# Cross-attention block on one Trainium2 core: low score products in one run, context in bank 3, low masks first, empty PE instructions shared between W2 and W1

## The chip, the cores and the metric

The kernel runs on one NeuronCore of a Trainium2 chip. The metric is the device time of one execution in microseconds. Before the change the median of 3 runs is 1749.11 us (1749.05 to 1751.23). TensorE is called PE here, VectorE DVE, ScalarE ACT, GpSimd POOL; SP issues most DMAs.

## What is computed

A cross-attention block with its feed-forward part, in fp32, for 128 sequences of 128 tokens, 256 features, 16 heads of 16, and 1024 hidden units. The reference, cut to what matters:

```python
q, k, v = query @ Wq + bq, key @ Wk + bk, values @ Wv + bv   # split into 16 heads
scores = einsum('bhqd,bhkd->bhqk', q, k) / sqrt(16)
scores = where(j < i, scores, -1e30)          # a query sees earlier keys only
attn = softmax(scores); attn[:, :, 0, :] = 0  # the first query sees none
x = layer_norm(query + ctx @ Wo + bo, ln1_g, ln1_b)
ffn = relu(x @ W1 + b1) @ W2 + b2
out = layer_norm(x + ffn, ln2_g, ln2_b)
```

## The kernel before

The work goes in 64 pairs of sequences, p = 0 to 63. All five engines follow an order written out by hand: a function call in the kernel adds its instructions to each engine's queue at that place, and a tile framework adds only the semaphore waits. Pairs 0 to 4 have orders of their own (the start, `third`, `fourth`, `fifth`); from p = 5 on `step(p)` is called for each pair, and at the end `behind` twice and a few calls more. The pipeline is deep: `step(p)` computes the context of pair p-2, scores and softmax of pair p, the queries and keys of p+1, the hidden layer of p-3 and the second feed-forward product of p-4.

On PE a step runs in this order: the context products (`weigh`, L583 and L594), the scores (`scores_both`), queries (L271, `xT,wq`), output projection (L614), keys (L271, `cT,wk`), values (L303), the second feed-forward product W2 (`second_by_seven`, L891), and the hidden layer W1 (`hidden`, L801). An fp32 matmul is carried out as two matmul instructions with a weight load each, so counts in the profile are twice those in the order.

The scores use the mask. Query rows 64 to 127 are two groups of 32 (g = 2 with 96 keys, g = 3 with 128 keys), called high (HI); rows 0 to 63 are one group with 64 keys, called low (LO, g = 0). Low products are 16 matmuls of 64 rows (`low_products`, L423), high ones 16 for each g of 32 rows (`group_scores`, L406). Each uses a strip of 32 of PE's rows (`strips`, r = 0 to 3). Four of the eight PSUM banks hold the high scores (bank r for strip r), the other four the low ones (bank 4 + (r + 2) % 4). `scores_both` mixes them: low products of strips 2 and 3 for half of the heads, high ones of g = 3 in strips 0 and 1, low ones again, and so on.

DVE then adds the masks. For low scores `masked(p, 0, FORE)` reads banks 4 and 5 and `masked(p, 0, REAR)` banks 6 and 7 into SBUF (L455). For high ones `mask_high` adds the mask in place (L843) and takes each head's maximum from PSUM (L459), for strips 0 and 1 (FORE) or 2 and 3 (REAR). ACT takes the exponentials: 16 of the high heads straight from the banks, 16 of the low ones from SBUF (`exponential_by_head`, L857).

The banks are used again within a step: queries in bank 4, output projection in 5, keys in 0, values in 1, W1 in banks 2, 3, 4 and 0 in turn, W2 in 6 and 7, and `weigh` puts the context into bank 7, from where ACT copies it to `cxT` (`context`, L607). A matmul that writes a bank waits until the engine that read it last is done.

W2 multiplies by the 2 x 2 blocks of W2 in seven products of 4 matmuls (`product`), the four sums that it needs (`hS`) come from POOL (`combine_hidden`, L877 to L880), and DVE adds the products up (`sum_of_seven`, L920 and L928). After its matmuls stand empty instructions (`empty`, L225): 20 in each of five products and 19 in two, 138 in all, 5 after a matmul nearly everywhere. They compute nothing:

```python
    def empty(n):
        for _ in range(n):
            nc.tensor.nop(hint="pad", nofuse=True)
```

W2 is called this way 60 times, for pairs 3 to 62.

Of the kernel before, what the change touches and what calls it, by code (L numbers as in the profile page):

```python
# [13 lines left out]
P = 128  # L14
# [5 lines left out]
def tile_cross_attention_block(  # L20
# [162 lines left out]
    one = const.tile([1, P], F32, tag="one", name="one")  # L183
# [36 lines left out]
    def at_bank(i, name):  # L220
        return banks[:, i, :]
# [5 lines that stand above are left out]
    def bank(name):  # L227
        turns[0] += 1
        return at_bank(4 + turns[0] % 4, name)
# [185 lines left out]
    def low_products(p, strips=range(NS), ms=range(KC)):  # L415

        st = states[p]
        bank0 = 4 if p > 3 else 0
        for m in ms:
            for s in range(2):  # L420
                for r in strips:
                    strip, first = slice(32 * r, 32 * r + 32), s * P
                    nc.tensor.matmul(  # L423
                        banks[s * HP : (s + 1) * HP, bank0 + (r + 2) % 4, m * P : (m + 1) * P].rearrange(
                            "p (e j) -> p e j", e=2
                        ),
                        st["qT"][strip, m, first : first + HP],
                        st["kT"][strip, m, :, first : first + HP],
                        start=True, stop=True,
                    )  # L430

    def scores_both(p):

        one, two = (0, 1), (2, 3)
        low_products(p, two, (0,))
        group_scores(p, 3, one)
        low_products(p, two, (1,))
        group_scores(p, 3, two)
        group_scores(p, 2, one)
        low_products(p, one, (0,))  # L440
        group_scores(p, 2, two)
        low_products(p, one, (1,))

    def masked(p, g, at=slice(0, 4)):

# [11 lines left out]
    def largest(p, g, src=None, heads=slice(None)):  # L457
        src = weights(p, g) if src is None else src
        nc.vector.tensor_reduce(  # L459
            states[p]["nmx"][g][:, heads], src, AX.X, ALU.max, negate=True  # L460
        )
# [110 lines left out]
    def weigh(p):  # L572

        st = states[p]
        pT = st.pop("pT")
        pc = at_bank(7, f"pc_{p}") if p > 1 else bank(f"pc_{p}")
        new = p > 1

        for m in range(KC):
            for s in range(2):  # L580
                at = (m * 2 + s) * P
                for j in range(NS):
                    nc.tensor.matmul(  # L583
                        pc[32 * j : 32 * j + 32, at : at + HP],
                        st["vd"][:, s, 4 * m + j].rearrange("p e d -> p (e d)"),
                        pT[:, 2 * s : 2 * s + 2, 1, 2 * ((j + 2) % 4) + m, :] if new
                        else pT[:, 2 * s : 2 * s + 2, H + 2 * j + m, :],
                        start=True, stop=True,
                    )
            for s in range(2):  # L590
                at = (m * 2 + s) * P
                for e in range(2):
                    for j in range(NS):
                        nc.tensor.matmul(  # L594
                            pc[32 * j : 32 * j + 32, at + HP : at + P],
                            st["vz"][:, s, 4 * m + j, 2 * e : 2 * e + 2, :].rearrange(
                                "p e d -> p (e d)"
                            ),
                            pT[:, 2 * s + m, 0::2, 2 * j + e, :] if new
                            else pT[:, 2 * s : 2 * s + 2, 4 * j + 2 * m + e, :],  # L600
                            start=(e == 0), stop=(e == 1),
                        )
        st["pc"] = pc
# [186 lines left out]
    def hidden(p, fs, between=None):  # L790
        st = states[p]
        if fs[0] == 0:
            st["hT"] = ffn.tile([P, FC, TP], F32, tag="hT", name=f"hT_{p}", bufs=1)
        for f in fs[::2]:
            if p == 0:
                ph = bank(f"ph_{p}_{f}")
            else:
                ph = at_bank((2, 3, 4, 0)[f // 2], f"ph_{p}_{f}")
            for i in range(2):
                for k in range(KC):  # L800
                    nc.tensor.matmul(  # L801
                        ph[:, i * TP : (i + 1) * TP].rearrange("p (s i a) -> p s i a", s=2, a=32),
                        w1[:, k, (f + i) * P : (f + i + 1) * P], st["x1T"][:, :, :, k, :],
                        start=(k == 0), stop=(k == KC - 1),
                    )
            for i in range(2):
                nc.scalar.activation(  # L807
                    st["hT"][:, f + i, :], ph[:, i * TP : (i + 1) * TP], AF.Relu,
                    bias=(b1e_c if p else b1_c)[:, f + i : f + i + 1], scale=1.0,
                )  # L810
            if between:
                between(f)
# [36 lines left out]
    HI, LO = (3, 2), (0,)  # L849
# [11 lines left out]
    wt = const.tile([P, 4, FC // 2, P], F32, tag="wt", name="wt")  # L861
# [20 lines left out]
    def second_by_seven(p):  # L882

        st = states[p]
        hT, hs = st["hT"], st["hS"]
        py = st["py"] = at_bank(6, f"py_{p}")
        pz = st["pz"] = at_bank(7, f"pz_{p}")

        def product(out, left, right, after):
            for k in range(FC // 2):  # L890
                nc.tensor.matmul(  # L891
                    out, left(k), right(k), start=(k == 0), stop=(k == FC // 2 - 1)
                )
                empty(after // (FC // 2) + (after % (FC // 2) > k))

        def raw(e, s):
            return lambda k: hT[:, 2 * k + e, s * P : (s + 1) * P]

        def weights(e, h):
            return lambda k: w2[:, 2 * k + e, h * P : (h + 1) * P]  # L900

        product(py[:, :P], raw(0, 0), weights(0, 0), 20)
        product(pz[:, :P], raw(1, 0), weights(1, 0), 20)
        product(pz[:, 2 * P : 3 * P], raw(1, 1), lambda k: wt[:, 3, k], 20)
        product(py[:, 3 * P :], lambda k: hs[:, 0, k], lambda k: wt[:, 0, k], 20)
        product(py[:, 2 * P : 3 * P], lambda k: hs[:, 2, k], lambda k: wt[:, 2, k], 20)
        product(py[:, P : 2 * P], lambda k: hs[:, 1, k], lambda k: wt[:, 1, k], 19)
        product(pz[:, P : 2 * P], lambda k: hs[:, 3, k], weights(1, 1), 19)

    def sum_of_seven(p):  # L910

# [324 lines left out]
    def step(p):  # L1236
        last = p == NP - 1
        weigh(p - 2)
        context(p - 2)
        if p == 5:  # L1240
            second_sum(1)
        scores_both(p)
        if p > 6:
            combine_hidden(p - 4, POOL_ALONE)
        if p == 5:
            finish(0)
            store(0)
        add_bo(p - 1)
        load_ahead(p)
        for g in LO:  # L1250
            masked(p, g, FORE)
        mask_high(p, FORE)
        exponential_by_head(p, HI, ONES)
        mask_high(p, REAR)
        exponential_by_head(p, HI, TWOS)
        for g in LO:
            masked(p, g, REAR)
        for g in LO:
            largest(p, g)
        if p > 5:  # L1260
            exponential_by_head(p, LO, range(H))
        if not last:
            queries(p + 1)
        attention_out(p - 2)
        attention_sum(p - 2)
        attention_stats(p - 2)
        shift(p - 2, 1)
        norm1(p - 2)
        if not last:
            keys(p + 1)  # L1270
        if p == 5:
            exponential_by_head(p, LO, range(H))
        values(p)
        values_out(p)
        if p > 5:
            norm2(p - 5)
        divided(p, 3)
        divided(p, 2)
        divided(p, 0)
        turn_x1(p - 2)  # L1280
        residual1(p - 3)
        if p > 6:
            second_by_seven(p - 4)
        elif p == 6:
            second_half(2, 1)
        hidden(p - 3, range(FC // 2 if p == 5 else 0, FC))
        if p == 5:
            second_half(2, 0)
        if p + 2 < NP:
            tokens(p + 2, "x")  # L1290
            tokens(p + 2, "c")
        turned(p, 3)
        if p > 6:
            sum_of_seven(p - 4)
        for g in (2, 0):
            turned(p, g)
        brought(p, nc.sync, LATE_FIRST)
        if p > 5:
            finish(p - 5)
            store(p - 5)  # L1300
        stats(p - 4, states[p - 4]["t2"], 2)
        scale_and_shift(p - 4)
# [101 lines left out]
```

## Time and profile before

| what | value |
|---|---|
| median of 3 runs | 1749.11 us (1749.05 to 1751.23) |
| the profiled execution | 1748.55 us |
| its span, first to last instruction | 1746.8 us |
| granted PE clock | 0.997 of full speed |
| PE busy | 1722.8 us |
| DVE, ACT, POOL busy | 1271.8, 1103.6, 1246.9 us |
| DMA, mean | 110 GB/s |

A row of a timeline names the start and the length in us, the engine, the line, the operation, the tiles it writes and reads, their shape and the number of instructions merged in it; in brackets stands the engine's idle time before it and what ended that. Matmuls are pipelined and their ends are modelled, so a row's length reaches into the next row, and the difference of two starts is the better measure. `PEld` is PE's weight load; a `q` behind an engine's name is its sequencer.

### The profile page before, as it was taken

Reading aid. Unit: us, or ns where it says so; the run is one execution under the profiler, and the core shown is the slowest. Engines: PE = TensorE matmul, PEld = TensorE weight load, DVE = VectorE, ACT = ScalarE, POOL = GpSimd, SP = SyncE. Lnnn points to the kernel's source line nnn. Section 1 sums busy time; section 2 is a strip of 40 time slices with the busy share of each in tenths; the row PEclk is TensorE's granted clock in tenths of the full one; section 3 lists DMA queues with packets and bytes.
Section 4 is the critical chain, followed back from the end, with each engine's and each line's share of the span. In section 5 each row is a group of like instructions: output and inputs, shape, how many; then the busy total and the mean of one; then the engine's idle time right before and its main releaser. Section 6 shows DMA issues by size and latency. Waiting matters only on the chain.

```text
span 1746.8 us, 58786 instructions
## 1 busy us (share of the span) xinstructions
PE 1722.8 (99%) x19910; PEld 1419.0 (81%) x19910; DVE 1271.8 (73%) x2240; ACT 1103.6 (63%) x3391; POOL 1246.9 (71%) x1297
## 2 busy tenths in 40 slices
PE   8989999999999999999999999999999999999998
PEld 6767888888888888888888888888888888888787
DVE  7767787687777777866876877777778678778654
ACT  6556576676675665765766766656657667667542
POOL 7856776776777777767767767777777677677664
PEclk9999999999999999999999999999999999999999
DMA  8354455454454454454554554544545545543321
GB/s 176 81 119 114 115 116 122 109 114 113 106 119 116 110 119 104 110 124 109 117 113 104 115 122 108 119 106 108 121 113 113 114 105 119 123 105 92 95 64 43
DMA packets 415325, 192.75 MB, mean 110 GB/s; under 512 B 282448, under 2 KB 387024, under 8 KB 415056
## 3 DMA queue, kind: packets, MB, share of 16 engines
q1 hardware_dynamic: 413152, 188.03, 46.6%
q8 instruction: 189, 3.10, 0.8%
q10 hardware_dynamic: 1904, 0.96, 0.2%
q14 instruction: 80, 0.66, 0.1%
HBM read 70.26 MB, written 33.29 MB: 59 GB/s over the span
## 4 chain that ended last, share of the span: by engine, by line
PE 95%; DVE 1%; POOL 1%; ACT 1%; DMA 1%; issue 0%; SPq 0%; POOLq 0%; ACTq 0%; DVEq 0%
PE banks L891 27%; PE banks L801 26%; PE banks L271 13%; PE banks L614 6%; PE banks L303 6%; PE banks L406 5%; PE banks L423 5%; PE banks L594 3%; PE banks L583 2%; PE banks L819 0%; ACT sm L857 0%; DMA pT<-tb 0%; POOL sm L548 0%; DVE nmx L459 0%; SPq L506 0%
## 5 line engine op out<-in xcount | busy, mean ns | idle before, releaser
L801 PE MATMUL banks<-x1T,w 128*128 128x256 f32 x2048 | 458.0, 381 | 1.4 <-ACT kT L293 1.4
L801 PEld LDWEIGHTS banks<-x1T,w 128*128 128x128 f32 x2048 | 384.0, 190 | 59.4 <-ACT kT L293 1.8
L807 ACT ACTIVATE hT<-banks,b1e_c 128x256 f32<-128x256 f32 x504 | 211.4, 471 | 334.0 <-PE banks L801 334.0
L857 ACT ACTIVATE sm<-banks,nmx 128x128 f32<-128x128 f32 (+1 forms) x944 | 237.9, 402 | 200.6 <-DVE nmx L459 197.3
L482 POOL TENSOR_TENSOR sm<-sm,rs 128x1024 f32<-128x1024 f32 x186 | 321.9, 1758 | 7.7 <-ACT hT L807 4.9
L455 DVE TENSOR_TENSOR sm<-banks,neg 128x512 f32<-128x512 f32 (+1 forms) x122 | 84.8, 695 | 322.8 <-PE banks L423 322.8
L634 POOL TENSOR_SCALAR ve<-mv 128x2 f32<-128x2 f32 x127 | 29.3, 230 | 320.1 <-DVE mv L628 319.7
L857 ACT ACTIVATE sm<-sm,nmx 128x64 f32<-128x64 f32 x944 | 235.4, 434 | 0.0
L480 DVE TENSOR_REDUCE su<-sm 128x8 f32<-128x1024 f32 x186 | 205.2, 1103 | 32.7 <-ACT sm L857 26.6
L891 PE MATMUL banks<-wt,hS 128*128 128x128 f32 x1440 | 225.8, 293 | 0.0
L891 PEld LDWEIGHTS banks<-wt,hS 128*128 128x128 f32 x1440 | 191.3, 190 | 29.6 <-issue 0.5
L496 DVE STREAM_TRANSPOSE tb<-sm 128x1024 f32<-128x1024 f32 x186 | 204.2, 1125 | 0.0
L877 POOL TENSOR_TENSOR hS<-hT 128x512 f32<-128x512 f32 x57 | 72.5, 1272 | 104.3 <-ACT hT L807 104.3
L459 DVE TENSOR_REDUCE nmx<-banks 128x4 f32<-128x512 f32 x236 | 136.4, 620 | 4.1
L271 PE MATMUL banks<-xT,wq 128*128 128x256 f32 x504 | 127.0, 395 | 2.9 <-DVE sm L455 2.9
L293 ACT ACTIVATE kT<-banks,bkh,half 128x256 f32<-128x256 f32 x252 | 125.7, 636 | 3.9 <-PE banks L271 3.9
L303 PE MATMUL banks<-wv,cT 128*128 128x256 f32 x512 | 121.1, 379 | 1.0 <-ACT sm L857 1.0
L891 PEld LDWEIGHTS banks<-w,hT 128*128 128x128 f32 x960 | 117.6, 192 | 4.6 <-issue 0.5
L614 PE MATMUL banks<-wo,cxT 128*128 128x256 f32 x512 | 121.2, 379 | 0.0
L271 PE MATMUL banks<-cT,wk 128*128 128x256 f32 x504 | 119.3, 379 | 1.3 <-DVE sm L455 1.3
L891 PE MATMUL banks<-w,hT 128*128 128x128 f32 x960 | 119.5, 276 | 0.2
L406 PE MATMUL banks<-kT,qT 32*32 32x192 f32 (+1 forms) x3968 | 115.6, 360 | 0.6 <-ACT hT L807 0.6
(139 smaller groups left out, 3124.6 us busy)
## 6 DMA issues: line engine op xcount, KB each, us to landing
pT<-tb SPq DMA_DIRECT2D x738, 96.0 KB, 2.2
x1t<-tbx SPq DMA_DIRECT2D x252, 64.0 KB, 1.8
x1T<-x1t SPq DMA_DIRECT2D x63, 256.0 KB, 2.8
out_dram<-t SPq DMA_DIRECT2D x63, 256.0 KB, 2.4
xb<-in_x_dram SPq DMA_DIRECT2D x124, 128.0 KB, 4.1
cb<-in_ctx_dram SPq DMA_DIRECT2D x124, 128.0 KB, 4.3
x<-in_x_dram SPq DMA_DIRECT2D x31, 512.0 KB, 5.3
pT<-tb SPq DMA_DIRECT2D x123, 64.0 KB, 2.0
```

Source lines behind the costliest of these rows:

```text
L271: nc.tensor.matmul(ps[:, m * TP : (m + 1) * TP], w[:, k, m * P : (m + 1) * P], src[:, k, :], start=(k == 0), stop=(k == KC - 1),)
L303: nc.tensor.matmul(pv[:, s * D : (s + 1) * D], st["cT"][:, k, s * P : (s + 1) * P], wv[:, k, :], start=(k == 0), stop=(k == KC - 1),)
L406: nc.tensor.matmul(banks[32 * c : 32 * c + 32, r].rearrange("p (e x) -> p e x", e=2)[:, :, WITHIN[g] : WITHIN[g] + n], st["qT"][strip, m, ...
L459: nc.vector.tensor_reduce(states[p]["nmx"][g][:, heads], src, AX.X, ALU.max, negate=True)
L480: nc.vector.tensor_reduce(st["su"][g], sm, AX.X, ALU.add)
L482: nc.gpsimd.tensor_tensor(sm, sm, per_head(p, g, "rs"), ALU.mult)
L496: nc.vector.transpose(to, sm)
L614: nc.tensor.matmul(po[:, s * D : (s + 1) * D], cxT[:, k, s, :], wo[:, k, :], start=(k == 0), stop=(k == KC - 1),)
L801: nc.tensor.matmul(ph[:, i * TP : (i + 1) * TP].rearrange("p (s i a) -> p s i a", s=2, a=32), w1[:, k, (f + i) * P : (f + i + 1) * P], st[ ...
L807: nc.scalar.activation(st["hT"][:, f + i, :], ph[:, i * TP : (i + 1) * TP], AF.Relu, bias=(b1e_c if p else b1_c)[:, f + i : f + i + 1], sc ...
L857: nc.scalar.activation(sm[:, h], src, AF.Exp, bias=states[p]["nmx"][g][:, h : h + 1], scale=1.0)
L891: nc.tensor.matmul(out, left(k), right(k), start=(k == 0), stop=(k == FC // 2 - 1))
```

## The change

Four edits. `scores_both` issues all low products first, then the high ones of g = 3 and of g = 2, each in strips 0 to 2 and then strip 3. From p = 3 on `weigh` puts the context into bank 3 instead of bank 7. In `step` DVE adds the low masks of both halves before the high ones, and takes the low maximum after the high ones. And W2 has 10 empty instructions in each product, 70 in all, while W1 gets 4 after each of its 16 matmuls from p = 4 on, and one more after the first four: 68. A step has 138 before and after.

```diff
     def scores_both(p):
 
-        one, two = (0, 1), (2, 3)
-        low_products(p, two, (0,))
-        group_scores(p, 3, one)
-        low_products(p, two, (1,))
-        group_scores(p, 3, two)
-        group_scores(p, 2, one)
-        low_products(p, one, (0,))
-        group_scores(p, 2, two)
-        low_products(p, one, (1,))
+        low_products(p)
+        for g in HI:
+            for strips in ((0, 1, 2), (3,)):
+                group_scores(p, g, strips)
...
-        pc = at_bank(7, f"pc_{p}") if p > 1 else bank(f"pc_{p}")
+        pc = at_bank(3 if p > 2 else 7, f"pc_{p}") if p > 1 else bank(f"pc_{p}")
...
+                    if p > 3:
+                        empty(4 + (2 * (f + i) + k < 4))
...
-        product(py[:, :P], raw(0, 0), weights(0, 0), 20)
+        product(py[:, :P], raw(0, 0), weights(0, 0), 10)
...
-        product(pz[:, P : 2 * P], lambda k: hs[:, 3, k], weights(1, 1), 19)
+        product(pz[:, P : 2 * P], lambda k: hs[:, 3, k], weights(1, 1), 10)
...
-        for g in LO:
-            masked(p, g, FORE)
+        masked(p, 0, FORE)
+        masked(p, 0, REAR)
         mask_high(p, FORE)
         exponential_by_head(p, HI, ONES)
         mask_high(p, REAR)
         exponential_by_head(p, HI, TWOS)
-        for g in LO:
-            masked(p, g, REAR)
-        for g in LO:
-            largest(p, g)
+        largest(p, 0)
```

PE, the scores of one pair in the middle of the run, before: behind the last context products (`vz`) stand eight pieces, low (64x128) and high (32x2x128 for g = 3, 32x2x96 for g = 2) in turn, and then the queries.

```order
L594 MATMUL banks<-pT_199,vz_191 32x64 x16
L423 MATMUL banks<-kT_15479,qT_15449 64x128 x4
L406 MATMUL banks<-kT_15479,qT_15449 32x2x128 x8
L423 MATMUL banks<-kT_15479,qT_15449 64x128 x4
L406 MATMUL banks<-kT_15479,qT_15449 32x2x128 x8
L406 MATMUL banks<-kT_15479,qT_15449 32x2x96 x8
L423 MATMUL banks<-kT_15479,qT_15449 64x128 x4
L406 MATMUL banks<-kT_15479,qT_15449 32x2x96 x8
L423 MATMUL banks<-kT_15479,qT_15449 64x128 x4
L271 MATMUL banks<-xT_15710,wq 128x256 x4
```

The same place now:

```order
L589 MATMUL banks<-pT_199,vz_191 32x64 x16
L423 MATMUL banks<-kT_15479,qT_15449 64x128 x16
L406 MATMUL banks<-kT_15479,qT_15449 32x2x128 x16
L406 MATMUL banks<-kT_15479,qT_15449 32x2x96 x16
L271 MATMUL banks<-xT_15710,wq 128x256 x4
```

The same matmuls stand in three pieces. PE's passage from W2 (`hS`, the sums) to W1 (`x1T`) in the same step, before:

```order
L891 MATMUL banks<-w_136,hS_15392 128x128
L225 NO_OP x5
L891 MATMUL banks<-w_136,hS_15392 128x128
L225 NO_OP x4
L801 MATMUL banks<-x1T_15047,w_128 128x256 x16
```

And now:

```order
L888 MATMUL banks<-w_136,hS_15392 128x128
L225 NO_OP x2
L888 MATMUL banks<-w_136,hS_15392 128x128
L225 NO_OP x2
L796 MATMUL banks<-x1T_15047,w_128 128x256
L225 NO_OP x5
L796 MATMUL banks<-x1T_15047,w_128 128x256
L225 NO_OP x5
```

About half of the empties have moved from between W2's matmuls to between W1's. DVE at the start of a pair's softmax, before: the first low mask (`neg`), the high masks (`diag`) with their maxima, the second low mask and the low maximum, then the attention sum.

```order
L455 TENSOR_TENSOR sm_14016<-banks,neg 128x512
L843 TENSOR_TENSOR banks<-banks,diag 128x8x32
L459 TENSOR_REDUCE nmx_14017<-banks 128x4 x2
L843 TENSOR_TENSOR banks<-banks,diag 128x8x32
L459 TENSOR_REDUCE nmx_14017<-banks 128x4 x2
L455 TENSOR_TENSOR sm_14016<-banks,neg 128x512
L459 TENSOR_REDUCE nmx_14017<-sm_14016 128x16
```

And now:

```order
L450 TENSOR_TENSOR sm_14016<-banks,neg 128x512 x2
L840 TENSOR_TENSOR banks<-banks,diag 128x8x32
L454 TENSOR_REDUCE nmx_14017<-banks 128x4 x2
L840 TENSOR_TENSOR banks<-banks,diag 128x8x32
L454 TENSOR_REDUCE nmx_14017<-banks 128x4 x2
L454 TENSOR_REDUCE nmx_14017<-sm_14016 128x16
```

The second low mask has moved ahead of both high ones.

More of the change, by code (lines that the diff above doesn't have):

```diff
@@ L900, in weights @@
             return lambda k: w2[:, 2 * k + e, h * P : (h + 1) * P]
-        product(py[:, :P], raw(0, 0), weights(0, 0), 20)
[L903 to L907, printed above, removed]
-        product(pz[:, P : 2 * P], lambda k: hs[:, 3, k], weights(1, 1), 19)
+        product(py[:, :P], raw(0, 0), weights(0, 0), 10)
+        product(pz[:, :P], raw(1, 0), weights(1, 0), 10)
+        product(pz[:, 2 * P : 3 * P], raw(1, 1), lambda k: wt[:, 3, k], 10)
+        product(py[:, 3 * P :], lambda k: hs[:, 0, k], lambda k: wt[:, 0, k], 10)
+        product(py[:, 2 * P : 3 * P], lambda k: hs[:, 2, k], lambda k: wt[:, 2, k], 10)
+        product(py[:, P : 2 * P], lambda k: hs[:, 1, k], lambda k: wt[:, 1, k], 10)
+        product(pz[:, P : 2 * P], lambda k: hs[:, 3, k], weights(1, 1), 10)
     def sum_of_seven(p):
```

## The prediction, on record before the result was known

> **What bounds the kernel now.** I read the page first, then the timeline of TensorE (PE) over one step in the middle of the run, then VectorE (DVE) and ScalarE (ACT) over the same step.
>
> ```profile
> span 1746.8 us, 58786 instructions
> PE 1722.8 (99%) x19910; PEld 1419.0 (81%) x19910; DVE 1271.8 (73%) x2240; ACT 1103.6 (63%) x3391; POOL 1246.9 (71%) x1297
> q8 instruction: 189, 3.10, 0.8%
> ```
>
> PE is busy for 99% of the span, no other engine for more than 73%. So the time is the sum of PE's pieces, and the question is which of them are longer than their work. The timeline of PE for one step (columns: start, length, line, names, count; an fp32 matmul shows as two instructions, and lengths of neighbours overlap, so I use differences of starts):
>
> ```profile
> 906.11 0.45 PE L423 MATMUL banks<-kT,qT 32*64 32x128 f32 x8
> 906.49 0.66 PE L406 MATMUL banks<-kT,qT 32*32 32x256 f32 x16
> 907.08 0.45 PE L423 MATMUL banks<-kT,qT 32*64 32x128 f32 x8
> 907.46 0.66 PE L406 MATMUL banks<-kT,qT 32*32 32x256 f32 x32
> 908.05 0.52 PE L423 MATMUL banks<-kT,qT 32*64 32x128 f32 x8
> ...
> 909.36 1.99 PE L271 MATMUL banks<-xT,wq 128*128 128x256 f32 x8
> ...
> 912.91 1.89 PE L271 MATMUL banks<-cT,wk 128*128 128x256 f32 x8
> ...
> 916.37 1.95 PE L891 MATMUL banks<-w,hT 128*128 128x128 f32 x16
> 918.15 1.06 PE L891 MATMUL banks<-wt,hT 128*128 128x128 f32 x8
> 919.04 3.71 PE L891 MATMUL banks<-wt,hS 128*128 128x128 f32 x24
> 922.59 1.61 PE L891 MATMUL banks<-w,hS 128*128 128x128 f32 x8
> 924.16 7.14 PE L801 MATMUL banks<-x1T,w 128*128 128x256 f32 x32
> 931.23 0.43 PE L583 MATMUL banks<-pT,vd 128*32 128x64 f32 x16
> ```
>
> Two places stand out. The scores take 909.36 - 906.11 = 3.25 us in pieces of alternating shape. And the seven W2 products (L891) slow down as they go: 16 instructions in 1.78 us (0.111 each), 8 in 0.89, then 24 in 3.55 (0.148), the last 8 in 1.57 (0.196), all of one size. W2 takes 924.16 - 916.37 = 7.79 us; W1 (L801) takes 931.23 - 924.16 = 7.07 us, 0.44 for each of its 16 matmuls.
>
> **Why W2 slows: the empty instructions.** All of them stand in W2 now:
>
> ```profile
> L225 PEldq NOP  x8280: 13/13/13, 168.4 to 1727.2; - x198
> ```
>
> 8280 at 138 a call are 60 calls. They run on PE's sequencer (the q in PEldq), which also hands out the matmuls. At the start of W2 PE still has matmuls handed out in advance; when these are used up, it gets a new one only after five empties. The end of the run, where W2 follows the small context products directly, shows the slow pace almost from the start:
>
> ```profile
> 1676.75 2.96 PE L891 MATMUL banks<-w,hT 128*128 128x128 f32 x16
> 1679.62 1.65 PE L891 MATMUL banks<-wt,hT 128*128 128x128 f32 x8
> 1681.24 4.78 PE L891 MATMUL banks<-wt,hS 128*128 128x128 f32 x24
> ...
> 1687.30 1.97 PE L614 MATMUL banks<-wo,cxT 128*128 128x256 f32 x8
> ```
>
> Here 8 instructions take 1.62 us, 0.405 per matmul with its five empties, against 0.223 at the unslowed 0.111. The profile shows 13 ns of each empty and not what it holds up the sequencer for, so I bound that: if all of the 0.405 were empties, 0.081 us each; if they only add to the matmul, (0.405 - 0.223)/5 = 0.036. I take the upper end, as it is the harsher one.
>
> **The change part by part: W2 and W1.** W2 keeps 70 empties on 28 matmuls, 2.5 each: 2.5 x 0.081 = 0.203 us, below the 0.223 that PE needs. W1 gets 68 on 16 matmuls, 4.25 each: 0.344 us, below its 0.44. So the sequencer stays ahead of PE in both, and the empties cost nothing while that holds; the matmuls themselves hide them. The margin in W2 is thin (9%), but in W1 it is 22%. W2 at the full rate: 56 x 1.78/16 = 6.23 us, a gain of 7.79 - 6.23 = 1.56 us in a step. Steps 7 to 63 have it: 57 x 1.56 = 88.9 us. The three calls at the end (10.55 us from 1676.75 to 1687.30) could gain 4.3 us each, 12.9 in all, but there W2 waits for its own sums hS from GpSimd and VectorE sooner; I take 10 and keep 0 to 12.9. Together 98.9 us.
>
> **The scores.** The count of matmuls stays: 32 low and 64 high instructions a step. What goes is the alternation. A piece of 8 low instructions takes 0.38 us (906.11 to 906.49), yet all 32 take little more in one run, as an early step shows, where the low and the high products stand ungrouped as the change has them:
>
> ```profile
> 43.73 0.69 PE L423 MATMUL banks<-kT,qT 32*64 32x128 f32 x32
> 44.35 1.99 PE L801 MATMUL banks<-x1T,w 128*128 128x256 f32 x8
> ```
>
> ```profile
> 61.63 1.39 PE L406 MATMUL banks<-kT,qT 32*32 32x256 f32 x64
> 62.94 0.48 PE L819 MATMUL banks<-w,hT 128*128 128x256 f32 x1
> ```
>
> 32 low ones in 0.62 us and 64 high ones in 1.31 us: 1.93 us where 3.25 are spent, 1.32 less. Bounds: 16 high ones alone took 0.59 us (906.49 to 907.08) and 32 together also 0.59 (907.46 to 908.05), so 64 cost 1.18 to 2.36 us, and the scores 1.80 to 2.98. I take 1.93, the same instructions in nearly the same order. 57 x 1.32 = 75.2 us. Steps 4 to 6 have the new scores too, but wait for other things; at most 4 us there.
>
> **Bank 3 and the context.** The context products now go to bank 3, and the high scores of strip 3 must wait until ACT has copied them out. Bank 7, which the low products need at once, is then held by W2's sums alone, and VectorE has read those before the row at 928.52 below, 3 us ahead of the next scores.
>
> ```profile
> 906.29 0.58 ACT L607 COPY cxT<-banks 128x508 f32<-128x508 f32 x1 [0.71 <-ACT hT L807]
> ...
> 910.19 4.03 ACT L857 ACTIVATE sm<-banks,nmx 128x128 f32<-128x128 f32 x16 [3.32 <-DVE nmx L459]
> ...
> 926.22 0.84 ACT L807 ACTIVATE hT<-banks,b1e_c 128x256 f32<-128x256 f32 x2 [2.46 <-PE banks L801]
> ```
>
> Counted from the first score, S = 906.11, the copy ends at S + 0.76. Strip 3 comes after 32 low and 24 high instructions, at S + 0.62 + some 0.1: a wait of 0 to 0.1 us, at most 6 us over the run; I take 0, because the other strips have work until then. The Trainium skill (TensorE: Matmul & The Clock Gate, Part 3, on what overlaps) says that matmuls start strictly in program order, so that all behind the waiting one would wait as well; by that rule the sum would be the 6 us dearer. No row here shows a wait inside the scores that would tell.
>
> **VectorE's new order.** It adds the low masks of both halves first, then the high ones:
>
> ```profile
> 907.66 0.69 DVE L455 TENSOR_TENSOR sm<-banks,neg 128x512 f32<-128x512 f32 x1 [5.60 <-PE banks L423]
> 908.45 0.43 DVE L843 TENSOR_TENSOR banks<-banks,diag 128x256 f32<-128x256 f32 x1
> ...
> 928.52 0.18 DVE L628 BATCH_NORM_AGGREGATE mv<-bs 128x2 f32<-128x6 f32 x1
> ...
> 934.26 0.69 DVE L455 TENSOR_TENSOR sm<-banks,neg 128x512 f32<-128x512 f32 x1 [5.56 <-PE banks L423]
> ```
>
> A step is 934.26 - 907.66 = 26.60 us. The first low mask starts 0.58 after the second low piece (907.08) begins; 32 low instructions end 0.24 later than 8 (0.69 against 0.45), so it starts at S + 0.82. Two masks of 0.69 put the high mask at S + 2.20 (today 908.45, S + 2.34). The exponentials follow 1.74 later as today (910.19 - 908.45), at S + 3.94, and free bank 0 after four of sixteen, 1.0 us, at S + 4.95. The key projection, which writes bank 0, stands 912.91 - 909.36 = 3.55 after the queries, so at S + 1.93 + 3.55 = S + 5.48. It has 0.5 us to spare, today 1.7. The queries need the first low mask out of bank 4: S + 1.51, before S + 1.93.
>
> **The other engines.** The step becomes 26.60 - 1.56 - 1.32 = 23.7 us. VectorE's softmax work starts some 1.2 us later against PE, so of its 5.56 idle us 5.56 - 2.9 - 1.2 = 1.5 are left; ACT's idle time before the hidden layer (2.46) shrinks to about 1.3 by the same delay. Neither becomes the bound. What is late next is bank 0.
>
> **The sum.** The profiled execution took 1748.55 us (span 1746.8), the median is 1749.11. 1748.55 - 98.9 - 75.2 = 1574.4; with the 0.56 between them, 1575.
>
> **The rivals.**
>
> *Bank 0 becomes the wait.* If VectorE or ACT loses more than 0.5 us after the scores, the keys wait for the exponentials, and each 0.1 us is 5.7 us over the run. For it: the margin falls from 1.7 to 0.5, and the high mask also needs three quarters of the high scores. Against: ACT's own pace (4.03 for sixteen) stays. A wait of 0.3 to 1.0 us gives 1592 to 1632. Chance 0.11.
>
> *The scores gain nothing.* Directly behind the context products the sequencer may have no lead, and the pieces could be paced by that rather than by the changes of shape: 1650. Against: they follow them today, and the first low piece (0.38 us) is no longer than the later ones. Chance 0.08.
>
> *W2 gains nothing.* If an empty holds up the matmuls around it wherever it stands, W1 loses what W2 wins: 1748.55 - 75.2 = 1673. Against: W2's first 24 instructions run at 0.111 with empties between them. Chance 0.05.
>
> *Another chain holds the step at 26.6 us,* and nothing changes: 1749. It would need VectorE's 5.56 idle us to be gone by latency. Chance 0.03.
>
> *Slower: code loading.* q8 brought 189 pieces of 16 KB; 0.8% of 16 engines x 1746.8 us / 189 is 1.18 us each, about three a step. The change moves the empties, and so moves where in the step the pieces are asked for: one that fell at W1, whose matmuls last 0.44 us, may fall to the small products, which eat instructions far faster. Three exposed pieces cost 3.5 us a step against 2.9 won: 57 x 0.6 = 34 us, 1783. It decides from 2.9 us of exposed loading a step. Against: the number of instructions per step stays the same, and PE's rows above show no gap of that length although some three pieces come in each step. The Trainium skill (Advanced Engine Details and Errata, ISA Cache) gives 256 instructions to a 16 KB line and only two lines; the trace agrees on the size (3.10 MB in 189). Chance 0.03.
>
> **How the numbers follow.** The forecast has 0.70. Its own range goes from 1560 (scores at 1.80 us, 7 us; the end's 2.9; steps 4 to 6, 4) to 1635 (scores at 2.98, 60 us). With the first rival, which ends inside it, I give 1555 to 1640, which leaves out the other rivals' 0.19. A change under 0.2% (3.5 us) can't be told from none here. Faster: 0.70 + 0.11 + 0.08 + 0.05 = 0.94; same 0.03; slower 0.03.
>
> **What would show it.** W2 at 0.111 us to its last eight instructions, and W1 still at 7.1; one low and one high piece of scores, 1.9 us together; a step of 23.7 us; the keys starting without a wait for ACT. Wrong would be: W2 still slowing at its end; W1 longer; PE idle ahead of the keys or in the scores; a PE share well under 99%.

## The result and the profile after

The median is 1577.6 us (4 runs, 1575.86 to 1577.88) beside 1750.17 us for the kernel before (4 runs): a ratio of 0.9011, 95% interval 0.8995 to 0.9026, 172.6 us less. The forecast was 1575. From the page of the changed kernel:

```profile
span 1576.2 us, 58785 instructions
PE 1544.0 (98%) x19910; PEld 1361.7 (86%) x19910; DVE 1253.1 (80%) x2240; ACT 1095.4 (69%) x3391; POOL 1246.4 (79%) x1297
q8 instruction: 189, 3.10, 0.9%
```

PE is still the bound, with 178.8 us less of busy time, while DVE, ACT and POOL do what they did before in a shorter time. One step of PE's timeline:

```profile
689.42 2.00 PE L271 MATMUL banks<-xT,wq 128*128 128x256 f32 x8
...
692.98 1.89 PE L271 MATMUL banks<-cT,wk 128*128 128x256 f32 x8
...
696.44 1.95 PE L888 MATMUL banks<-w,hT 128*128 128x128 f32 x16
...
699.11 2.84 PE L888 MATMUL banks<-wt,hS 128*128 128x128 f32 x24
701.79 1.06 PE L888 MATMUL banks<-w,hS 128*128 128x128 f32 x8
702.69 7.07 PE L796 MATMUL banks<-x1T,w 128*128 128x256 f32 x32
709.69 0.43 PE L578 MATMUL banks<-pT,vd 128*32 128x64 f32 x16
...
711.17 0.69 PE L423 MATMUL banks<-kT,qT 32*64 32x128 f32 x32
711.79 1.39 PE L406 MATMUL banks<-kT,qT 32*32 32x256 f32 x64
713.11 1.13 PE L271 MATMUL banks<-xT,wq 128*128 128x256 f32 x4
```

W2's last 24 and 8 instructions take 2.68 and 0.90 us (before 3.55 and 1.57), one pace from the first to the last. No row of this step has a bracket: PE waits for nothing. Step by step beside the forecast:

| | before | forecast | after |
|---|---|---|---|
| W2 | 7.79 | 6.23 | 702.69 - 696.44 = 6.25 |
| W1 | 7.07 | 7.07 | 709.69 - 702.69 = 7.00 |
| scores | 3.25 | 1.93 | 713.11 - 711.17 = 1.94 |
| step | 26.60 | 23.7 | 713.11 - 689.42 = 23.69 |

DVE and then ACT behind those scores (S = 711.17):

```profile
712.04 1.29 DVE L450 TENSOR_TENSOR sm<-banks,neg 128x512 f32<-128x512 f32 x2 [2.41 <-ACT cxT L602]
713.24 0.42 DVE L840 TENSOR_TENSOR banks<-banks,diag 128x256 f32<-128x256 f32 x1
```

```profile
714.97 4.02 ACT L854 ACTIVATE sm<-banks,nmx 128x128 f32<-128x128 f32 x16 [3.03 <-DVE nmx L454]
```

The first low mask starts at S + 0.87 (forecast 0.82), the high mask at S + 2.07 (2.20), the exponentials at S + 3.80 (3.94). Bank 0 is free when the fourth of the sixteen ends, 1.09 us after the first starts in the trace's single rows, at S + 4.89; the keys start 692.98 - 689.42 = 3.56 behind the queries, S + 5.50. About 0.6 us are to spare, where the forecast had 0.5. At the end stand three W2 calls behind the last step. The second and the third come to wait for POOL, the third longest:

```profile
1515.66 2.05 PE L888 MATMUL banks<-w,hT 128*128 128x128 f32 x16
...
1522.02 1.89 PE L609 MATMUL banks<-wo,cxT 128*128 128x256 f32 x8
...
1553.67 2.05 PE L888 MATMUL banks<-wt,hS 128*128 128x128 f32 x16 [1.88 <-POOL hS L875]
```

The first takes 6.36 us in place of 10.55; the other two take 7.0 and 8.7 with their waits, in place of 10.6 and 10.4. That is 9.4 us less together, where the forecast took 10.

### The profile page after: what moved, and what is told of

Its sections match the earlier page's. It is cut to its first block, busy times and chain, and to the rows that moved or that the text cites. A ratio compares the mean times of both kernels' runs of the same rounds, so it can differ in the third digit from the quotient of the medians.

```text
span 1576.2 us, 58785 instructions
## 1 busy us (share of the span) xinstructions
PE 1544.0 (98%) x19910; PEld 1361.7 (86%) x19910; DVE 1253.1 (80%) x2240; ACT 1095.4 (69%) x3391; POOL 1246.4 (79%) x1297
## 4 chain that ended last, share of the span: by engine, by line
PE 91%; POOL 3%; DVE 2%; ACT 1%; issue 1%; DMA 0%; SPq 0%; POOLq 0%; DVEq 0%; ACTq 0%
PE banks L796 26%; PE banks L888 23%; PE banks L271 14%; PE banks L609 7%; PE banks L303 6%; PE banks L406 5%; PE banks L589 4%; PE banks L423 2%; PE banks L578 2%; POOL sm L477 0%; POOL sd L630 0%; ACT sm L854 0%; POOL pT L367 0%; DVE sm L450 0%; POOL sm L543 0%
## 5 line engine op out<-in xcount | busy, mean ns | idle before, releaser
L450 DVE TENSOR_TENSOR sm<-banks,neg 128x512 f32<-128x512 f32 (+1 forms) x122 | 79.8, 694 | 148.2 <-ACT cxT L602 128.0
L888 PE MATMUL banks<-wt,hS 128*128 128x128 f32 x1440 | 171.2, 276 | 2.3 <-POOL hS L875 2.3
L888 PEld LDWEIGHTS banks<-wt,hS 128*128 128x128 f32 x1440 | 165.8, 192 | 2.6 <-POOL hS L875 2.6
L271 PEld LDWEIGHTS banks<-xT,wq 128*128 128x128 f32 x504 | 92.0, 192 | 31.8 <-issue 16.2
L303 PEld LDWEIGHTS banks<-wv,cT 128*128 128x128 f32 x512 | 97.4, 191 | 15.2 <-ACT sm L854 2.4
```

Source lines behind the costliest of these rows:

```text
L271: nc.tensor.matmul(ps[:, m * TP : (m + 1) * TP], w[:, k, m * P : (m + 1) * P], src[:, k, :], start=(k == 0), stop=(k == KC - 1),)
L303: nc.tensor.matmul(pv[:, s * D : (s + 1) * D], st["cT"][:, k, s * P : (s + 1) * P], wv[:, k, :], start=(k == 0), stop=(k == KC - 1),)
L888: nc.tensor.matmul(out, left(k), right(k), start=(k == 0), stop=(k == FC // 2 - 1))
```

## The experiments

The theory: W2 gains because PE's sequencer, which hands out matmuls and empties alike, no longer falls behind the matmuls; the scores gain because PE changes tile shape three times and not eight. The rivals: an empty costs wherever it stands; bank 0, bank 3 or DVE's new order decides; the code's 16 KB pieces are what was moved. A further rival, that the scores gain by having more strips at work at a time, has no run of its own.

### The empties alone

```diff
 kernel before:
+                    if p > 3:
+                        empty(4 + (2 * (f + i) + k < 4))
...
-        product(py[:, :P], raw(0, 0), weights(0, 0), 20)
+        product(py[:, :P], raw(0, 0), weights(0, 0), 10)
```

> The kernel before with the empties alone shared between W2 and W1 (70 and 68 a call); scores, bank of the context products and VectorE's order as before. If an empty costs nothing as long as the sequencer's time for a matmul and its empties stays below the matmul's own time: W2 at 0.111 us per instruction to its end, 6.25 us instead of 7.79, W1 7.0, a step of 25.0 us, some 1652 us (97 less than before). If an empty holds up the matmuls beside it wherever it stands: W1 grows by what W2 loses, a step of 26.6, 1749 us.

Measured: 1647.74 us, ratio 0.9416 (0.9402 to 0.9430), 102.4 less; steps of 24.99 us. W1 with its 68 empties:

```profile
728.32 7.07 PE L801 MATMUL banks<-x1T,w 128*128 128x256 f32 x32
735.33 0.43 PE L583 MATMUL banks<-pT,vd 128*32 128x64 f32 x16
```

7.01 us, no more than without any, and W2 takes 6.25. An empty does not cost where the sequencer is ahead, and the rival that it costs wherever it stands is out. Against the changed kernel this one has the old scores, the context in bank 7 and the old order of masks: 24.99 - 23.69 = 1.30 us a step is what the new scores are worth together with these two.

### The scores, bank 3 and the masks alone

```diff
 changed kernel:
-                    if p > 3:
-                        empty(4 + (2 * (f + i) + k < 4))
...
-        product(py[:, :P], raw(0, 0), weights(0, 0), 10)
+        product(py[:, :P], raw(0, 0), weights(0, 0), 20)
```

> The changed kernel with all 138 empties back in W2; the scores in two pieces, the context products in bank 3 and VectorE's new order stay. If the changes of shape cost the scores 1.3 us whatever stands elsewhere: scores 1.94 us, W2 7.8, a step of 25.25 to 25.3 us, some 1674 us. If the two parts of the change help each other (the shorter scores only paying with the sequencer ahead), scores over 2.2 us and more than 1690. If they overlap, less than 1665.

Measured: 1693.53 us, ratio 0.9669 (0.9652 to 0.9685): 56.6 less and not 75. The steps are 25.55 us in the mean. The time lies in the second case (over 1690), the scores in the first: they do take 1.94 (754.95 to 756.89). It is W2 that does not take what it took:

```profile
738.38 1.95 PE L886 MATMUL banks<-w,hT 128*128 128x128 f32 x16
...
741.06 3.92 PE L886 MATMUL banks<-wt,hS 128*128 128x128 f32 x24
744.82 1.61 PE L886 MATMUL banks<-w,hS 128*128 128x128 f32 x8
746.40 7.15 PE L796 MATMUL banks<-x1T,w 128*128 128x256 f32 x32
```

W2 takes 746.40 - 738.38 = 8.02, 0.23 more than in the kernel before. The empties of one step (first and last start) show why, in this kernel and in the one before:

```profile
L225 PEldq NOP  x138: 13/13/13, 735.4 to 746.2; - x138
```

```profile
L225 PEldq NOP  x138: 13/13/13, 912.9 to 924.0; - x138
```

The first empty stands behind W2's first matmul and tells when the sequencer has handed that out: 738.38 - 735.4 = 3.0 us ahead here, 916.37 - 912.9 = 3.5 before. The sequencer stops ahead of the keys at a semaphore that DVE's first high maxima raise. Since the scores are shorter, that comes 1.78 us behind the start of the queries and not 0.76, and the first empty comes 2.2 us after it, in this kernel as in three others where it was raised at 1.77, 1.87 and 3.04. So the shorter scores take half a microsecond from the sequencer's advance; with five empties a matmul W2 pays for it, with 2.5 it doesn't. The two parts alone give 102.4 + 56.6 = 159.0 us, together 172.6.

### All empties in W1

```diff
 changed kernel:
-                        empty(4 + (2 * (f + i) + k < 4))
+                        empty(8 + (2 * (f + i) + k < 10))
...
-        product(py[:, :P], raw(0, 0), weights(0, 0), 10)
+        product(py[:, :P], raw(0, 0), weights(0, 0), 0)
```

> The changed kernel with all 138 empties behind W1's matmuls (8 or 9 each), none in W2. If the sequencer's advance is what counts: W2 6.25 us; an empty at 0.071 to 0.081 us makes 0.65 to 0.70 us per matmul of 0.44, 10.3 to 11.2 us for W1, started up to 3.6 us ahead (32 instructions of W2), so W1 0 to 0.6 us longer and the small context products, which follow without an advance, 0 to 0.5 us longer: a step of 23.7 to 24.8 us. If empties cost by their number alone: 23.7. If W1 shows the whole of it: 27 us or more.

Measured: 1720.09 us (one run), steps of 26.1 us in the mean, outside every case. PE's timeline and then its weight loads:

```profile
756.00 8.79 PE L796 MATMUL banks<-x1T,w 128*128 128x256 f32 x32
765.19 0.43 PE L578 MATMUL banks<-pT,vd 128*32 128x64 f32 x16 [0.41 <-DMA pT<-tb]
```

```profile
759.57 0.30 PEld L796 LDWEIGHTS banks<-x1T,w 128*128 128x128 f32 x2 [0.36 <-issue]
760.26 0.30 PEld L796 LDWEIGHTS banks<-x1T,w 128*128 128x128 f32 x2 [0.39 <-issue]
760.92 0.30 PEld L796 LDWEIGHTS banks<-x1T,w 128*128 128x128 f32 x2 [0.36 <-issue]
761.53 0.30 PEld L796 LDWEIGHTS banks<-x1T,w 128*128 128x128 f32 x2 [0.32 <-issue]
762.12 0.30 PEld L796 LDWEIGHTS banks<-x1T,w 128*128 128x128 f32 x2 [0.29 <-issue]
```

W1 takes 9.19 us. After its first eight matmuls each waits for `issue`, the sequencer: two gaps with 9 empties make (760.92 - 759.57)/2 = 0.675 us a matmul, the next two, with 8, make (762.12 - 760.92)/2 = 0.600, so about 0.07 us for an empty and 0.03 for the matmul. The expected price was right. What was wrong is the advance: I had taken 32 instructions of W2, 3.6 us. The empties here start at 754.2, 756.00 - 754.2 = 1.8 us ahead of W1's first matmul: 1.8/0.111 = 16 instructions. The changed kernel shows the same 1.75 us at nearly every matmul of the second half of W2, so 16 is how far the sequencer gets. Eight matmuls use it up: each loses 0.675 - 0.44 = 0.24, eight lose 1.9. Not the number of empties but their spread decides: the same 138 cost nothing shared, 1.6 us in W2, 2.2 in W1.

### The low maximum ahead of the high masks

```diff
 changed kernel:
         masked(p, 0, REAR)
+        largest(p, 0)
         mask_high(p, FORE)
...
-        largest(p, 0)
```

> The changed kernel with VectorE's maximum over the low scores (1.21 us) moved ahead of the high masks, which comes 1.1 us later by it. The trace after shows bank 0 free 0.6 us ahead of the key products. If that is the margin, the keys wait 0.5 us in each step: 24.2 us, some 1606 us in all. If nothing waits for the exponentials, 23.7 and 1578. If more than bank 0 hangs on it (the sequencer stands at a semaphore ahead of the keys until the first high maxima are there, and loses its advance), over 24.5.

Measured: 1627.71 us (one run), steps of 24.53. The keys, and the list of who waits for whom (us in total, times, longest):

```profile
710.37 1.89 PE L609 MATMUL banks<-wo,cxT 128*128 128x256 f32 x8
712.80 1.99 PE L271 MATMUL banks<-cT,wk 128*128 128x256 f32 x8 [0.54 <-ACT sm L854]
```

```profile
PE banks L271 <- ACT sm L854: 31.8, 57, 0.9
```

In each of 57 steps the keys wait for the exponentials. They start 712.80 - 710.37 = 2.43 us behind the output projection in place of 692.98 - 691.26 = 1.72, and the values follow 1.83 behind them in place of 1.73, as PE restarts: 0.81. The exponentials came 1.25 us later, not 1.1, which the expectation had worked out from the maximum's length. 1.25 less 0.6 to spare, and the 0.10, make 0.75 of the 0.81. The mean step lies just over the 24.5 of the third case, but not by its mechanism: W2, which would pay for a lost advance, takes 6.25 us here too. Bank 0 is next in line, with a margin close to the forecast.

### DVE's old order

```diff
 changed kernel:
         masked(p, 0, FORE)
-        masked(p, 0, REAR)
         mask_high(p, FORE)
...
         exponential_by_head(p, HI, TWOS)
+        masked(p, 0, REAR)
         largest(p, 0)
```

> The changed kernel with VectorE's order as before: the second low mask (0.69 us) behind the high masks. The exponentials come 0.65 us earlier against the scores, so bank 0 is free 1.2 us ahead of the keys instead of 0.6, and nothing else waits for the second low mask (bank 5 is needed by the attention output, bank 6 and 7 by W2, 7 us after the queries start). If VectorE's new order is worth nothing: a step of 23.69 us, 1577 us (within 0.2%). If the new order is needed: the attention output or W2 starts late, a step over 23.8, over 1583 us. If it costs something: under 1573.

Measured: 1578.09 us, ratio 0.9016 (0.9002 to 0.9029); steps of 23.69. The new order is worth nothing. DVE in this kernel:

```profile
709.81 0.69 DVE L450 TENSOR_TENSOR sm<-banks,neg 128x512 f32<-128x512 f32 x1 [2.42 <-ACT cxT L602]
711.00 0.43 DVE L840 TENSOR_TENSOR banks<-banks,diag 128x256 f32<-128x256 f32 x1 [0.50 <-PE banks L406]
```

My reason was wrong, though: the exponentials don't come earlier. The high mask waits 0.50 us for the high scores and starts 1.19 us behind the first low mask, 1.20 in the change. The second low mask (0.69) fills that wait and no more.

### All four strips in turn

```diff
 changed kernel:
-            for strips in ((0, 1, 2), (3,)):
+            for strips in (range(NS),):
```

> The changed kernel with the high scores of strip 3 no longer set behind those of the other three strips but in turn with them. Then the second or third high matmul already writes bank 3, out of which ScalarE copies the context products until 0.77 us after the first score, and the first high instruction starts at 0.62. If matmuls start strictly in order: the high scores stand until 0.82, 0.1 to 0.2 us a step, 23.8 to 23.9 us, 1583 to 1589. If the other strips go on past the waiting one: 23.69, 1577. If the two pieces of the strips cost more by themselves than the wait (they leave TensorE with one strip to work on): under 23.6 us, under 1573.

Measured: 1586.46 us, ratio 0.9060 (0.9045 to 0.9074), 8.4 us over the kernel of the previous experiment on the same chip; steps of 23.84.

```profile
711.68 1.54 PE L406 MATMUL banks<-kT,qT 32*32 32x256 f32 x64
713.15 1.99 PE L271 MATMUL banks<-xT,wq 128*128 128x256 f32 x8
```

The high scores take 1.47 us, 0.15 more: the wait for the copy, as strict order has it. Setting strip 3 last hides it.

### The context left in bank 7

```diff
 changed kernel:
-        pc = at_bank(3 if p > 2 else 7, f"pc_{p}") if p > 1 else bank(f"pc_{p}")
+        pc = at_bank(7, f"pc_{p}") if p > 1 else bank(f"pc_{p}")
```

> The changed kernel with the context products left in bank 7. The low products of strip 1 write bank 7, and are the second of each four, so nearly all low products stand behind ScalarE's copy, which ends 0.77 us after the first score. With matmuls in strict order the scores last 1.94 + 0.65 to 0.8 us: steps of 24.3 to 24.5 us, 1612 to 1624 us. If the copy is early enough or the other strips go ahead: 23.7 to 23.9, 1577 to 1590.

Measured: 1622.95 us (one run), steps of 24.51.

```profile
727.02 0.43 PE L423 MATMUL banks<-kT,qT 32*64 32x128 f32 x2
727.83 0.69 PE L423 MATMUL banks<-kT,qT 32*64 32x128 f32 x30 [0.39 <-ACT cxT L602]
```

Strip 0's first product (two instructions) starts, strip 1's waits 0.81 us for the copy, and the other 28 instructions, of which those of strips 0, 2 and 3 write other banks, stand behind it. This is the rule of the Trainium skill (TensorE: Matmul & The Clock Gate, Part 3) that matmuls start in program order, and this trace agrees. Bank 3 is worth 0.82 us a step of the 1.30: without it, low products in one run would gain 0.5.

### No empties

```diff
 changed kernel:
-                    if p > 3:
-                        empty(4 + (2 * (f + i) + k < 4))
...
-        product(py[:, :P], raw(0, 0), weights(0, 0), 10)
+        product(py[:, :P], raw(0, 0), weights(0, 0), 0)
```

> The changed kernel with no empties in W2 and W1 at all: 630 instructions a step in place of 768, so that the 16 KB pieces of code (256 instructions) begin at another place of each step. If loading is hidden wherever a piece begins (a piece lasts at least 2.1 us at the sequencer's 8.3 ns per instruction, and takes 1.2 us to come): all steps 23.7 us, 1575 to 1578. If a piece that begins in the small products (384 of the 630 instructions) holds up TensorE: steps of different length, 0 to 2.4 us longer, 24.0 to 25.5 us in the mean, 1595 to 1680 us.

Measured: 1605.68 us, ratio 0.9161 (0.9141 to 0.9180), 28 us slower than with them. Of 55 steps 28 last 23.7 us, the others up to 25.5. One of those:

```profile
721.90 0.82 PE L406 MATMUL banks<-kT,qT 32*32 32x256 f32 x28
723.86 1.13 PE L406 MATMUL banks<-kT,qT 32*32 32x256 f32 x36 [1.14 <-issue]
724.92 3.50 PE L271 MATMUL banks<-xT,wq 128*128 128x256 f32 x8
```

PE stands in the middle of the scores for `issue`: the sequencer has nothing to hand out. A step of 630 instructions moves the beginnings of the 256-instruction pieces of code by 118 from step to step, so they pass through all places. That the gaps belong to these beginnings can be counted. In 21 of the 55 steps over half a microsecond lies between two starts in the high scores or ahead of the queries. Over all of PE's records in order of time, these 21 places are 1280, 3072 or 4352 instructions apart, each time a multiple of 256.

### Pieces of code moved by 128, 64 and 192 instructions

```diff
 changed kernel (the third, half a piece; also with 64 and with 192):
         last = p == NP - 1
+        if p == 7:
+            empty(128)
         weigh(p - 2)
```

> The changed kernel with 128 empties put once ahead of the first step with W2, so that from there on each 16 KB piece of code begins half a piece earlier: at the end of W2, in the context products and at the end of the scores. They cost up to 9 us once. If loading is hidden wherever a piece begins: steps of 23.69 us, at most 1587 in all. If a piece that begins in the small products is exposed: up to 1.2 us a step, 24.0 to 24.9 us, 1595 to 1655.

> The changed kernel with 64 empties once ahead of the first step with W2, so that each 16 KB piece of code begins a quarter of a piece earlier (pieces would begin in W2, in W1's last matmuls or the first context products, and in the first half of the scores). With half a piece the last of the three began shortly before the end of the scores and stood there for 1.2 us in each step. If only a short stretch behind another piece's beginning is exposed: 23.69 us. If any place in the small products is: 24.0 to 25.2.

> The changed kernel with 192 empties once at the same place: pieces begin three quarters of a piece earlier, or one quarter later, than in the change. Same two cases: 23.69 us, or 24.0 to 25.2 where a piece begins within about 2.5 us of the sequencer's way behind another one.

Measured, one run each: 1651.62, 1584.90 and 1595.11 us; steps of 24.90 in the mean, 23.70 and 23.70. With 64 and 192 the rest is paid once, around the place of the added empties. With 128 every step pays. The scores there, and the list of waits:

```profile
643.42 1.19 PE L406 MATMUL banks<-kT,qT 32*32 32x256 f32 x41
645.77 0.59 PE L406 MATMUL banks<-kT,qT 32*32 32x192 f32 x23 [1.15 <-issue]
646.28 1.99 PE L271 MATMUL banks<-xT,wq 128*128 128x256 f32 x8
```

```profile
PE banks L406 <- issue: 46.3, 56, 1.2
```

In each of 55 steps the gap stands ahead of the same instruction of the high scores, and its length differs (0.63 to 1.49 us between two starts): something that comes late, not work. From gap to gap PE's records count 768, again a multiple of 256, and the place within the 256 is that of the gaps without empties. So a piece whose first instruction stands there is not hidden; a quarter of a piece to either side all are.

### The kernel before, moved likewise

```diff
 kernel before:
         last = p == NP - 1
+        if p == 7:
+            empty(128)
         weigh(p - 2)
```

> The kernel before with the same 128 empties once, so that its pieces of code begin where those of the half-piece kernel do. If the place of the pieces is as costly to the kernel before, its step grows by about the same 1.2 us: 27.8 us, some 1820. If its longer scores (3.25 us in place of 1.94) give the piece the time to come: 26.6 us, 1750 to 1760. The change's gain would then depend on the place of the pieces: 2.9 us where they are, 1.7 half a piece away.

Measured: 1782.02 us (one run), steps of 27.03 in the mean, 0.43 over its own 26.60: between the two cases. The last high piece of a step, in the kernel before and in this run:

```profile
908.49 0.56 PE L406 MATMUL banks<-kT,qT 32*32 32x192 f32 x16
908.98 0.45 PE L423 MATMUL banks<-kT,qT 32*64 32x128 f32 x8
```

```profile
713.37 1.00 PE L406 MATMUL banks<-kT,qT 32*32 32x192 f32 x16
714.30 0.45 PE L423 MATMUL banks<-kT,qT 32*64 32x128 f32 x8
```

It takes 0.93 us in place of 0.49. The slower scores of before hide most of the piece, not all. At this place the change would be worth 27.03 - 24.90 = 2.1 us a step and not 2.9.

## Why the prediction was right, and where it was not

**W2, forecast 1.56 us a step, measured 1.54.** The mechanism is shown: the parts alone, the empties' spread and the sequencer's advance all fit. The upper end that I took for an empty, 0.081 us, is 0.07 by the W1 run; the lower bound of 0.036 is out. The trace of before could have told: most neighbouring empties start 0.070 or 0.071 us apart there. The margin is as thin as I called it, 2.5 x 0.07 + 0.03 = 0.205 against 0.223, and it is enough. It shows matmul by matmul, in how far the first empty behind a matmul starts ahead of that matmul on PE: before 3.4 us at W2's first, 1.8 at the ninth and nothing from the nineteenth on; now 3.0 at the first and 1.7 to 1.8, some 16 instructions, from the ninth to the last.

**W1, forecast unchanged, measured 0.07 less.** Its first weight load no longer comes late behind W2's last matmul: it starts 0.11 us ahead of W1's first matmul and not 0.03, and the second matmul instruction follows the first by 0.22 us and not 0.29.

**The scores, forecast 1.32, measured 1.31.** The row of an early step with the same order was the right measure. That it is the order together with bank 3 is shown by the runs: 0.82 of it is lost with the context in bank 7, and 0.15 with strip 3 in turn. What in the order does it is not separated. I named the changes of shape, but a piece of before also had two of the four strips at work, where the low products now have all four and the high ones three. The prediction's own rows show that this counts: 16 high instructions in two strips take 0.59 us (906.49 to 907.08), and 32, of which the second half is in the other two strips, take 0.59 as well (907.46 to 908.05). So the 1.31 is not the price of five changes of shape alone, and how it divides stays open.

**The wait for bank 3, put at 0.** By the trace's single rows the wait is there: the copy ends at S + 0.77, and strip 3's first instruction starts at S + 0.82, 0.11 behind the one before it. But nothing comes later by it. Of the two instructions of each matmul, the second ones of the other strips start 0.24 us behind the first ones, as they do in the kernel before. Bank 7 was no limit either: the row at 928.52 lies 4.2 us ahead of the next scores (906.11 + 26.60), more than the 3 us of the prediction.

**What the sum left out.** It added two terms as if they were independent. They are not: alone they give 159 us. It came out right because it costed W2 at the full rate, which needs the sharing all the more with the shorter scores.

**DVE's reserve was mis-sized.** The step on the other engines said that 5.56 - 2.9 - 1.2 = 1.5 us of idle time would be left. The row shows 2.41 ahead of the scores alone. A later start against PE moves the idle time and doesn't use it, so the 1.2 should not have been taken off.

**The end, forecast 10, measured 9.4,** and steps 4 to 6, for which the range had up to 4 us, gave nothing (0.9 us more). The 2.6 us between 1575 and 1577.6 I don't resolve in full. In the profiles 2.3 us stand ahead of the steps: the first queries start 8.0 us behind the first instruction before and 10.3 after. In the runs of this study that start lies between 8.0 and 10.6, and why is open.

**The rivals.** Bank 0 did not bind, and would from 0.6 us on. That scores or W2 gain nothing, or that another chain holds the step, is excluded by the first two runs. The slower case, code loading, did not come about, but its mechanism is real and I had the wrong reason against it. I argued that the number of instructions per step is unchanged, and that about three pieces a step leave no gap. The number alone does not protect: with the same number and the pieces half a piece away each step loses 1.2 us. And 1.18 us, the time of a piece's packets, is not the price. In the moved kernel the piece that starts to come during the context or low products has landed 1.2 to 1.6 us before PE goes on, by the records of that queue, so more than the transfer lies between asking and running. The kernel would still have been faster, by some 100 us: in none of its steps, nor of those without empties, did more than one piece hold PE up. What in the sequencer takes the rest of the time stays open.

The Trainium skill (Runtime: NRT & Kernel Launch, Instruction fetch mechanics) says that the fetch of code is mostly hidden, because the sequencer hands out more slowly than pieces arrive. The traces agree for the place where the change has them, and not for the place half a piece away, where 46.3 us are spent waiting.

## What to carry to other kernels

Empty instructions cost nothing as long as the sequencer's time for a matmul and the empties behind it stays below the matmul's own; so spread them over the long matmuls and read from their starts how far the sequencer is ahead. Group small products by tile shape with all strips at work, and give the operation just ahead of them a bank that they need last, since all matmuls behind a waiting one stand too. After any edit that moves the number of instructions in PE's stream, look for `issue` waits in the small products before judging the edit, for the place where a piece of code begins can be worth as much as an edit: 1.2 us a step here, beside 1.3 for the scores.

## What the runs showed of the hardware

An empty on PE's sequencer is shown with 13 ns and takes about 70 of its time. The sequencer gets 16 matmul instructions ahead of PE in W2 (1.75 us at 0.111), no further. And in a few steps a gap in PE's work was followed by a lower clock, twice in the run without empties. After the 1.14 us wait in the scores shown there, the eight instructions of the queries took 3.29 us and not 1.83. The windows view of the stretch (busy time of PE, its weight loads, DVE, ACT and POOL, then PE's granted clock, the share of DMA and GB/s):

```profile
723.00:724.90 1.90, 1.04 (x36) 0.55 (x35) 0.53 (x2) 0.00 (x0) 1.90 (x2) 1.00 0.48 114
724.90:728.50 3.60, 3.60 (x10) 2.93 (x10) 3.53 (x7) 1.96 (x9) 2.71 (x3) 0.55 0.53 125
```

The granted clock is 0.55 for 3.6 us. The other time it is 0.51 from 1500.0 to 1503.5, behind a wait of 1.24 us. In the moved kernel before it is 0.50 from 768.9 to 772.3, behind only 0.55 us between two starts. Other gaps of the run without empties, one of them longer (1.41 us), and 55 of like length in the changed kernel with its pieces half a piece away were not followed by it, so what sets it off is open.
